# A graph layer with segment maxima: an evenly cut gather list, the bias in another product, and an end in smaller pieces

## The chip, the cores and the metric

The kernel runs on one core of one Trainium2 chip. The metric is the device time of one execution in microseconds (us); lower is better. Its engines are TensorE (PE, with PEld for its weight loads), VectorE (DVE), ScalarE (ACT), GpSimd (POOL) and SyncE (SP, which here only starts DMAs). Each engine works through its own queue in order, and they wait for each other by semaphores.

## The reference

There are 6,250 nodes with 256 features and 100,000 directed edges, sorted by target. For each edge a message is computed, each node takes the maximum of its messages, and the sum with x is normalised:

```python
x_src = x[src]; x_dst = x[dst]
theta_x = (x_dst - x_src) @ theta_w.T + theta_b
phi_x = x_src @ phi_w.T + phi_b
e = relu(theta_x + phi_x)
out = segment_max(e, dst, num_segments=6250)
x = layernorm(x + where(isfinite(out), out, 0.0))
```

The part of a message that depends on the target is the same for all edges of a node. So with b = x @ (phi_w - theta_w)^T and a = x @ theta_w^T, a node's result is relu(a[node] + max over its edges of b[src] + both biases). One row of b for each node suffices, and the work is to take maxima over gathered rows of b.

## The kernel before

**Two parts.** The first 18,688 edges (128 partitions x `T1` = 146 steps) belong to part 1, nodes 0 to 1,129. Each partition walks its own 146 edges: an indirect DMA on GpSimd gathers 128 rows (one step), and VectorE runs a capped maximum over the steps (`run`, L661). The running maxima go to a DRAM table, `maxima_1`, in groups of eight steps (L669); a node's result is read from the place of its last edge. Where a node's edges cross from one partition to the next, `tails_1` and `heads_1` mend the table: `heads_1` gathers the rows at the partitions' first boundaries, takes the maximum with what is carried over (L851) and scatters them back.

Part 2 are the other 5,120 nodes, 40 to a partition. Sources are cut into 17 slots of 375 nodes. For each node and slot one edge at most is chosen (`choice`), and its row comes by a product with a one-hot matrix on TensorE (`slot_part`, L1025): 85 parts of 24 matmuls, with one-hot matrices from ScalarE (L1017, L1018) and VectorE (L1015), and results joined into `acc` by VectorE (L1036). Edges that are left over form a list (`list_pieces`): each partition lists those of its own nodes, at most `LIST` = 288, and walks it as in part 1: 288 gathers (`gather_2`), 288 maxima, 36 writes to `maxima_2`.

**Preparation.** `b_of` transposes x on TensorE, copies it by ScalarE (`x_t`, L710), multiplies it (L720), and VectorE adds the bias and moves the result out of PSUM (L723). It does so for all rows (`b_rows`, in DRAM), and for the first `X_GROUPS` = 4 groups of part 1, whose rows of x are gathered directly since `b_rows` isn't there yet. Meanwhile VectorE fills a table of part 2's edges (`fill_table`), chooses, and forms the list. In the same loops `next_group_1` gathers the other groups of part 1 and starts the first 16 fetch parts.

**The list loop.** For each group of eight steps: eight gathers, the maxima of the group before, and `PACE` = 2.1 fetch parts:

```python
for i in range(LIST // STEPS):
    g, gathers = gather_2(i * STEPS)
    if i:
        run(2, g_before, STEPS, caps_2, (i - 1) * STEPS, maxima_2t, gathers)
    g_before = g
    pace += PACE
    fetch_parts(int(pace))
    pace -= int(pace)
    if i in (3, 5):
        next(heads, None)
```

The loop also finishes part 1's nodes (`rows_of`, `normalise`) in two shares, one node column and eight.

**The end.** Five shares of eight columns of part 2. `rows_of` loads x, gathers a node's row of `maxima_2` (L1127), and for each two columns (a piece) transposes x (L1134), copies it (L1136), multiplies it with theta (L1140), transposes `acc` back (L1149), and VectorE joins all (L1150, L1151, L1154). `normalise` then takes squares (L1165), the root, scales (L1172) and writes the output (L1176), a share behind `rows_of`.

**Order.** The order on each engine is fixed when the program is built, by a planner that places an instruction when its costs say that it can start. The kernel adds order by hand: `in_turn` keeps GpSimd's queue as written, with pauses (`iota` of 160) between gathers; `behind_in_order` places an instruction behind another without a wait. A `run` step of part 2 stands behind the gather of the next group and behind the last `acc` maximum written before it. If the limits of the tables don't hold (`bad`), a general path computes all once more at the end.

## Time and profile before

| what | value |
|---|---|
| median of 3 runs | 854.9 us (851.97 to 855.15) |
| the profiled execution | 852.55 us, its span 850.7 us |
| mean granted TensorE clock | 0.912 |
| PE, PEld busy | 663.9 us (78%), 537.1 us (63%) |
| DVE busy | 673.8 us (79%) |
| ACT busy | 497.8 us (59%) |
| POOL busy | 676.1 us (79%) |
| DMA | 178.69 MB, mean 210 GB/s |

All times are of one profiled execution, counted from the start of its span; the span is shorter than its time because starting and ending lie around it. Busy shares are means over stages that differ, so each stage is read by itself: which engine is full there, and what its successor waits for. Matmuls are pipelined, and a busy PE is not a PE at its peak. A line number names the line of the program that wrote the instruction; L497 is the helper that issues all indirect DMAs.

### The profile page before, as it was taken

What the parts mean: (1) busy time and instruction counts of PE and PEld (TensorE: products, weight loads), DVE (VectorE), ACT (ScalarE), POOL (GpSimd) and SP (SyncE); (2) the same over time, 40 slices, a digit from 0 to 9 for tenths busy, and PEclk for the clock granted to TensorE, in tenths of its full rate; (3) what the DMA queues carried; (4) which work ended last, traced back from release to release, by engine and by line L of the source; (5) the groups of instructions that cost most, each with busy time, mean ns of one, the idle gap of its engine ahead of it and who ended that gap; (6) DMA issues with size and microseconds to landing.
All of it is one profiled execution on the core that took longest, in us unless ns stands there. A gap on an engine that the chain in (4) does not pass through costs nothing. (4 is left out here: it accounts for less than half of the span.)

```text
span 850.7 us, 10236 instructions
## 1 busy us (share of the span) xinstructions
PE 663.9 (78%) x2949; PEld 537.1 (63%) x2949; DVE 673.8 (79%) x1227; ACT 497.8 (59%) x676; POOL 676.1 (79%) x913
## 2 busy tenths in 40 slices
PE   0899983767758285299999999999999999407771
PEld 0688862555536164288888888888888887306660
DVE  4599999977999872389988979888999978517662
ACT  0122224898749246077778868987777775004765
POOL 8796178887888788888888888888888888858820
PEclk9999995998879688599999999999999999758996
DMA  7675347776455663477778857986777667673622
GB/s 231 201 270 200 118 148 249 234 232 189 154 171 174 208 205 111 145 255 251 232 237 268 259 179 241 300 257 208 237 254 246 238 213 265 220 277 94 241 88 102
DMA packets 54353, 178.69 MB, mean 210 GB/s; under 512 B 12416, under 2 KB 13867, under 8 KB 45806
## 3 DMA queue, kind: packets, MB, share of 16 engines
q1 hardware_dynamic: 28306, 105.82, 35.0%
q0 software_dynamic: 23440, 64.42, 26.3%
q10 hardware_dynamic: 2540, 7.69, 2.4%
q8 instruction: 26, 0.43, 0.2%
q14 instruction: 41, 0.34, 0.1%
HBM read 107.88 MB, written 70.80 MB: 210 GB/s over the span
## 5 line engine op out<-in xcount | busy, mean ns | idle before, releaser
L1025 PE MATMUL ps_f<-hot,terms 128*128 128x512 f32 x2040 | 488.6, 400 | 74.5 <-DVE hot L1015 24.6
L1025 PEld LDWEIGHTS ps_f<-hot,terms 128*128 128x128 f32 x2040 | 390.9, 193 | 166.4 <-issue 25.0
L497 POOL DMA_INDIRECT g<-b_rows,list_src x288 | 293.4, 1019 | 50.0 <-issue 46.1
L1017 ACT ACTIVATE hot<-want,minus_row 128x1024 fp32r<-128x1024 f16 x186 | 204.9, 1145 | 133.4 <-PE ps_f L1025 128.5
L661 DVE SCALAR_TENSOR_TENSOR g<-g,caps 128x256 f32<-128x256 f32 x432 | 206.9, 479 | 31.2 <-DMA g<-b_rows,src 14.6
L1036 DVE TENSOR_TENSOR acc<-acc,ps_f 128x1024 f32<-128x1024 f32 x160 | 194.0, 1215 | 38.0 <-PE ps_f L1025 37.4
L497 POOL DMA_INDIRECT g<-b_rows,src x114 | 161.9, 1420 | 59.0 <-issue 29.6
L1018 ACT ACTIVATE hot<-hot 128x1024 fp32r<-128x1024 f32 x186 | 186.1, 1045 | 0.1
L473 POOL IOTA pause<- 128x160 f32 x404 | 125.2, 310 | 4.2
L720 PE MATMUL ps_b<-weights,x_t 128*128 128x256 f32 x324 | 75.8, 386 | 5.1 <-DVE b_sb L723 2.9
L720 PEld LDWEIGHTS ps_b<-weights,x_t 128*128 128x128 f32 x324 | 59.7, 190 | 17.8 <-ACT x_t L710 6.7
L710 ACT COPY x_t<-ps_xt 128x512 f32<-128x512 f32 (+1 forms) x41 | 21.9, 584 | 78.2 <-PE ps_xt L708 78.2
L497 POOL DMA_INDIRECT g<-maxima,place x49 | 48.3, 985 | 15.5 <-issue 15.0
L1140 PE MATMUL ps_e<-weights,x_t 128*128 128x256 f32 x160 | 42.7, 412 | 15.5 <-ACT x_t L1136 15.5
L1015 DVE TENSOR_SCALAR hot<-want,row_id 128x1024 fp32r<-128x1024 f16 x69 | 54.2, 785 | 0.5 <-DMA want<-chosen_rows 0.5
L1136 ACT COPY x_t<-ps_e 128x512 f32<-128x512 f32 x20 | 11.6, 581 | 58.4 <-PE ps_e L1134 58.3
L497 POOL DMA_INDIRECT g<-in_x_dram,src x32 | 38.9, 1215 | 8.7 <-issue 4.7
L1140 PEld LDWEIGHTS ps_e<-weights,x_t 128*128 128x128 f32 x160 | 30.3, 199 | 24.1 <-ACT x_t L1136 20.5
L1150 DVE TENSOR_TENSOR g<-g,ps_e 128x512 f32<-128x512 f32 x20 | 13.7, 686 | 32.1 <-PE ps_e L1149 18.8
L1134 PE MATMUL ps_e<-ident,g 128*128 128x128 f32 x80 | 13.2, 292 | 31.7 <-DVE g L1150 30.5
L1134 PEld LDWEIGHTS ps_e<-ident,g 128*128 128x128 f32 x80 | 10.4, 154 | 32.0 <-DVE g L1150 30.7
L1172 ACT ACTIVATE g<-g,r 128x256 f32<-128x256 f32 x49 | 25.3, 590 | 8.8 <-DVE r L1170 8.8
(210 smaller groups left out, 473.5 us busy)
## 6 DMA issues: line engine op xcount, KB each, us to landing
maxima<-g SPq DMA_DIRECT2D x54, 1024.0 KB
want<-chosen_rows SPq DMA_DIRECT2D x85, 256.0 KB
x_q<-in_x_dram SPq DMA_DIRECT2D x12, 512.0 KB
b_rows<-b_sb ACTq DMA_DIRECT2D x12, 512.0 KB
g<-in_x_dram SPq DMA_DIRECT2D x6, 1024.0 KB
out_dram<-g SPq DMA_DIRECT2D x6, 1024.0 KB
raw<-b_rows SPq DMA_DIRECT2D x16, 336.0 KB
g<-b_rows,list_src POOLq DMA_INDIRECT x288, 4.0
```

The costliest lines, as they stand in the source:

```text
L473: return nc.gpsimd.iota(t, pattern=[[step, t.shape[1]]], base=base, channel_multiplier=per_partition, allow_small_or_imprecise_dtypes=True,)
L497: in_turn(nc.gpsimd.indirect_dma_start(out=out, out_offset=out_offset, in_=in_, in_offset=in_offset))
L661: one = nc.vector.scalar_tensor_tensor(g[:, k, :], last[part], caps[:, t : t + 1], g[:, k, :], op0=ALU.min, op1=ALU.max)
L720: nc.tensor.matmul(ps[:, h, :], x_t[:, h, k, :], weights[:, k, 0, :], start=(k == 0), stop=(k == KC - 1))
L1015: nc.vector.tensor_scalar(hot[:, b, :], want, row_id[:, b : b + 1], None, op0=ALU.is_equal)
L1017: nc.scalar.activation(hot[:, b, :], want, AF.Abs, bias=minus_row[:, b : b + 1], scale=1.0)
L1018: nc.scalar.activation(hot[:, b, :], hot[:, b, :].bitcast(FP), AF.Relu, bias=1.0, scale=-1.0)
L1025: nc.tensor.matmul(ps[:, w : w + 512], terms[:, part, b, h * P : (h + 1) * P], hot[:, b, w : w + 512], start=(i == 0), stop=(i == n - 1),)
L1036: latest_part[0] = nc.vector.tensor_tensor(to, to, ps, op=ALU.max).ins.name
L1134: nc.tensor.transpose(ps[:, 2 * i + c, :], x_f[:, k + i, c * P : (c + 1) * P], ident)
L1140: nc.tensor.matmul(a[:, i, :], x_t[:, 2 * i + c, :], weights[:, c, 1, :], start=(c == 0), stop=(c == KC - 1))
L1172: nc.scalar.activation(x_f[:, k, :], x_f[:, k, :], AF.Identity, bias=mean[:, k : k + 1], scale=inv[:, k : k + 1])
```

## The change

- **Bias.** The sum of both biases is no longer added to b. It is kept in two rows (`bias_terms`, a rounded part and the rest) and added by one more matmul for each node column in `rows_of`, with `pick`, which selects these rows. `b_of` moves its result out of PSUM by a plain ScalarE copy.
- **Six groups of x**, not four, and a ring of six tiles, which the list's gathers share; x in `rows_of` has its own ring of five.
- **Equal chunks.** The partitions' lists are written to DRAM (`list_words`) and cut into 128 chunks of 231 places (`LIST_CHUNK`); a partition walks one chunk and up to 248 places, so that a node that begins in its chunk ends there too. A chunk is pieced together from three owners' lists with three run gathers and two masks. The loop has 31 groups instead of 36; `PACE` is 2.25. A group's maxima lie together in `maxima_2`. The places of nodes (`list_places`) are computed late in the loop.
- **Heads' maximum later.** The gather comes before group 2, the maximum before group 5 and behind the latest GpSimd instruction, the scatter before group 8.
- **The end.** Only part 1's single column is finished in the list loop, its eight others at the end. Pieces of two columns are begun one ahead of the one before; normalisation goes on in steps of two columns between them. The last share of eight is two of four.

The core of the diff (constants, table views, limits and buffers that are only renamed are left out):

```diff
-            nc.vector.tensor_tensor(to, ps[:, :n, :], bias.to_broadcast([P, n, D]), op=ALU.add)
+            nc.scalar.copy(to, ps[:, :n, :])
...
         indirect(heads, maxima_1, in_offset=at_heads)
-        nc.vector.tensor_tensor(heads, heads, carried, op=ALU.max)
         in_turn(iota(pause, 1, 0, 0))
+        yield
+        one = nc.vector.tensor_tensor(heads, heads, carried, op=ALU.max)
+        behind_in_order(one, latest[0], "rows that are there")
         yield
         indirect(maxima_1, heads, out_offset=at_heads)
...
+    def list_chunks():
+        ...
+        nc.tensor.matmul(ps[:, :P], counts, tri, start=True, stop=True)
+        nc.tensor.matmul(ps[:, P : P + 1], tri, n_list, start=True, stop=True)
+        nc.vector.tensor_copy(upper_end, ps[:, :P])
+        nc.vector.tensor_tensor(before, ps[:, P : P + 1], n_list, op=ALU.subtract)
+        ...
+        for i in range(3):
+            nc.vector.tensor_scalar(
+                scratch, upper_end, at_edge, None, op0=ALU.is_le, op1=ALU.add, accum_out=number[:, i : i + 1]
+            )
+            ...
+            nc.vector.scalar_tensor_tensor(up, scratch, FAR, upper_end, op0=ALU.mult, op1=ALU.add)
+            nc.vector.tensor_reduce(ends[:, i + 1 : i + 2], up, AX.X, ALU.min)
+            at_edge = ends[:, i + 1 : i + 2]
...
+        nc.vector.tensor_scalar(done, done, (1 << 20) - 1, None, op0=ALU.bitwise_and)
+        nc.vector.tensor_tensor(done, done, owner.to_broadcast([P, OWN_LIST]), op=ALU.bitwise_or)
+        for first_row, rows in ((0, P), (P, 3)):
+            nc.sync.dma_start(
+                flat(list_words, first_row * OWN_LIST, [[OWN_LIST, rows], [1, OWN_LIST]]), done[:rows, :]
+            )
+        yield
...
+        for i, to in enumerate((list_edges, second, third)):
+            gather_run(to, list_words, run_start[:, i : i + 1])
+        for i, to in enumerate((second, third)):
+            nc.vector.tensor_scalar(mask, edge, ends[:, i + 1 : i + 2], None, op0=ALU.is_ge)
+            nc.vector.copy_predicated(list_edges, mask, to)
...
-        g = ring_2.tile([P, STEPS, D], FP, name="g")
+        g = gathered.tile([P, STEPS, D], FP, name="g")
...
-        x_f = ring_2.tile([P, STEPS, D], FP, name="g")
+        x_f = x_ring.tile([P, STEPS, D], FP, name="x_f")
...
             nc.scalar.copy(x_t[:, : 2 * w], ps[:, : 2 * w])
+            yield
             a = ps_tile().rearrange("p (i d) -> p i d", i=2)
             for i in range(w):
                 for c in range(KC):
                     nc.tensor.matmul(
-                        a[:, i, :], x_t[:, 2 * i + c, :], weights[:, c, 1, :], start=(c == 0), stop=(c == KC - 1)
+                        a[:, i, :], x_t[:, 2 * i + c, :], weights[:, c, 1, :], start=(c == 0), stop=False
                     )
+                nc.tensor.matmul(a[:, i, :], pick, bias_terms, start=False, stop=True)
...
+    class Shares:
+        def step(self):
+            if self.begun is not None:
+                piece, norm = self.begun
+                next(piece)
+                self.begun = None
+                if norm is not None:
+                    self.norms.append(norm)
+                    return
+            for _ in range(2):
+                if self.norms and next(self.norms[0], self) is self:
+                    self.norms.pop(0)
+
+        def add(self, *share):
+            pieces, norm = rows_of(*share, self.ps_tile)
+            for i, piece in enumerate(pieces):
+                next(piece)
+                self.step()
+                self.begun = piece, norm if i == len(pieces) - 1 else None
...
     for i in range(LIST // STEPS):
+        if i in (2, 5, 8):
+            next(heads, None)
         g, gathers = gather_2(i * STEPS)
...
-        if i in (3, 5):
-            next(heads, None)
-        if i > 6 and i % 3 == 0 and (early_shares or waiting):
...
+        if i == LIST // STEPS - 4:
+            list_places()
+            early_share = Shares(misc)
+            early_share.add(*LAST)
+            early_share.finish()
...
+    last_shares = [(2, j, STEPS) for j in range(0, TILES - STEPS, STEPS)]
+    last_shares += [(2, j, STEPS // 2) for j in (TILES - STEPS, TILES - STEPS // 2)]
+    at_end = Shares(lambda: ps_end.tile([P, 2 * D], FP, name="ps_e"))
+    for share in [(1, 0, Q1)] + last_shares:
+        at_end.add(*share)
+    at_end.finish()
```

## The prediction

> **What bounds the kernel now.** First the page's forty slices of 21.3 us; a digit is the busy share in tenths.
>
> ```profile
> PE   0899983767758285299999999999999999407771
> DVE  4599999977999872389988979888999978517662
> POOL 8796178887888788888888888888888888858820
> ```
>
> Four stages: a preparation to about 300 us, where VectorE (DVE) is full; a list stage to 750, where GpSimd (POOL) never rests and TensorE (PE) is full after a hole; a gap; an end where nothing is full. The table of busy time by stretch (columns: span, then PE, PEld, DVE, ACT, POOL, granted clock, DMA share, GB/s) says the same in numbers:
>
> ```profile
> 255.00:300.00 45.00, 24.51 (x96) 18.11 (x94) 40.57 (x69) 27.43 (x28) 36.51 (x26) 0.80 0.56 187
> 300.00:355.00 55.00, 29.30 (x120) 23.47 (x120) 21.00 (x41) 22.15 (x23) 48.25 (x73) 0.75 0.47 142
> 355.00:722.00 367.00, 366.69 (x1614) 302.53 (x1614) 323.05 (x499) 278.20 (x298) 325.67 (x488) 0.99 0.75 244
> 722.00:757.00 35.00, 10.72 (x51) 8.46 (x50) 16.70 (x34) 1.76 (x3) 23.71 (x38) 0.70 0.61 210
> 757.00:834.00 77.00, 51.91 (x272) 42.55 (x272) 47.47 (x156) 42.62 (x117) 50.28 (x80) 0.89 0.47 168
> ```
>
> TensorE is done at 722; GpSimd gathers until 750, and the kernel waits. Who waits for whom names the holes:
>
> ```profile
> DVE heads L851 <- DMA heads<-maxima,head_i: 27.5, 1, 27.5
> PE ps_f L1025 <- DVE hot L1015: 24.6, 1, 24.6
> POOL g L497 <- DVE g L723: 23.4, 1, 23.4
> ```
>
> One VectorE instruction, the heads' maximum, waited from 324 to 351.6 for a gather that GpSimd reached at 348.9; everything behind it on VectorE stood, so TensorE stood 24.6. The third wait, 78 to 101.6, is GpSimd out of rows to gather. The costliest groups (busy us, mean ns) give prices:
>
> ```profile
> L497 POOL DMA_INDIRECT g<-b_rows,list_src x288 | 293.4, 1019 | 50.0 <-issue 46.1 <-DVE g L661 2.4 <-DVE acc L1036 0.8
> L661 DVE SCALAR_TENSOR_TENSOR g<-g,caps 128x256 f32<-128x256 f32 x432 | 206.9, 479 | 31.2 <-DMA g<-b_rows,src 14.6 <-DMA g<-b_rows,list_src 13.2
> L723 DVE TENSOR_TENSOR b_sb<-ps_b,bias 128x512 f32<-128x512 f32 (+1 forms) x25 | 16.6, 668 | 1.4 <-PE ps_b L720 1.4
> L723 DVE TENSOR_TENSOR g<-ps_b,bias 128x512 f32<-128x512 f32 x16 | 10.9, 682 | 1.0 <-PE ps_b L720 1.0
> ```
>
> Last, the chain that ended last (start us, us, what). It hangs on the list's last gather: its maximum, the write to `maxima_2`, then gathers held up beside 1 MB loads of x:
>
> ```profile
> 749.32 2.74 DMA g<-b_rows,list_src
> ...
> 752.15 0.49 DVE g L661
> 752.66 4.73 DMA maxima<-g
> 757.41 0.03 issue
> 757.44 8.27 DMA g<-in_x_dram
> 765.72 0.70 DVE g L1150
> ```
>
> The sum is made on the profiled execution: span 850.7, time 852.55, so 1.85 around it. It lies 2.35 below the median of 854.9.
>
> **Preparation.** Two chains must both be over before the first list gather (300.72 now).
>
> VectorE: 249 us busy of the 266 from 34.5 on. Taking the bias off removes its 41 evictions, which follow one another every 0.60 us (42.85, then 43.45): 24.6. ScalarE takes them: 49 copies at 0.58 (its 128x512 copy, L710) is 28 us on an engine that was busy 14 of 67 us there. If such a copy stands ahead of the next `x_t` copy, TensorE waits up to 1.2 for each of the 25 pairs of the main loop, 29 in all; cover is the 12 us by which the new x gathers outlast `b_rows`. VectorE gains work: `list_chunks` and two predicated copies, some 30 instructions of 0.15 to 0.5, about 6. And it gains a wait. The list goes through DRAM: two writes on SP, which may stand behind `maxima_1` writes (SP was held 10.2 us at 289), three run gathers on GpSimd at 1.4, and a landing (2.6 for the heads' gather). VectorE's predicated copies wait for that, with list words and `acc` maxima behind them; the list gathers wait too. No row shows this round trip. Below: 0, if other VectorE work and gathers fill it; above: 10.2 + 4.2 + 2.6 = 17. I take 9, near the heads' and run rows with a free SP. So 300.7 - 24.6 + 6 + 9 = 291, or 274 if the 17 us of idle goes too.
>
> As a page's figure: the Trainium skill, "DMA: Bandwidth & Descriptors", section "Anatomy of one DMA", speaks against round trips: about 2 us fixed for each transfer, mostly the receipt. Two legs by that are 4 where I have 9, and the time would be 5 shorter.
>
> GpSimd: 32 x gathers end at 78. Two more groups are 16 at 2.25 (20 took 45.1 from 33.2), so to 114, over the old hole. Then 98 gathers, not 114. They went at 1.746 ((300.72 - 101.65)/114): 171, to 285. At the stretch 170 to 213 (mean 1154 ns and 0.30 between) it is 257. TensorE's part of the two groups, eight pairs at 2.33, is 19; it ran to 124 and the first fetch part came at 143, so that is nearly covered.
>
> I take 284 for the first list gather, the slower GpSimd pace, and 262 to 302 as ends.
>
> The row behind the pace: gathers cost 1728 ns in 213 to 255, where VectorE was 100% busy with conversions and shifts, and 1018 in 352 to 725. The Trainium skill, "SBUF — State Buffer", section "Who interferes with whom", gives a mechanism: VectorE's two-port modes lock GpSimd out, and descriptors with it. By it the added masks, predicated copies and cast, some 2 us of VectorE, would block GpSimd for as long, and the time would be 2 longer; by the row all this sits in the 1.746.
>
> **List stage.** GpSimd: 299 indirect DMAs (288, nine for part-1 shares, two for the heads) took 300.7 to 750.6, 1.505 each. Now 248 + 1 + 2: 378, a gain of 72. TensorE decides beside it. ScalarE's one-hots mark the period of a fetch part:
>
> ```profile
> 319.84 2.20 ACT L1017 ACTIVATE hot<-want,minus_row 128x1024 fp32r<-128x1024 f16 x2 [1.35 <-PE ps_f L1025]
> 325.28 2.19 ACT L1017 ACTIVATE hot<-want,minus_row 128x1024 fp32r<-128x1024 f16 x2 [1.35 <-PE ps_f L1025]
> ```
>
> 5.44 a part. From 301.4 to 722.0 TensorE did 70 parts (380.8), the part-1 shares (11.7), stood 24.6 behind the heads, and 3.5 is left. The change puts the heads' maximum behind the gathers of three more groups and moves eight of the nine part-1 columns to the end: 380.8 + 1.6 + 3.5 = 386. A group is 8 x 1.505 = 12.0 on GpSimd and 2.25 x 5.44 = 12.2 on TensorE, so they end together, TensorE last: 284 + 386 = 670, GpSimd about 665. Hidden: 40 maxima less on VectorE (19 us at 479 ns), five 1 MB writes less, and `list_places`, a dozen small instructions at the 28th group; should VectorE lose its slack (88% busy), that is 3 us. A ring of six for the list, not seven that shares of x also used: GpSimd waited only 2.4 for a slot.
>
> **End.** The last eight maxima come behind the last part: 670 + 1.2 + 8 x 0.48 + 4.7 for the write is 680. Meanwhile GpSimd gathers the part-1 share (8 x 1.41 = 11.3, from 665). Part 2 needs two gathers and a landing, 5.4, and x lies loaded in five tiles of its own instead of coming just then: first maximum (L1150's) at 687, 765.7 now. Then twenty pieces. They went at 3.48 (19 steps from 765.72 to 831.83), because TensorE's transposes, the copy and the matmuls of a piece follow in line. Begun a piece ahead, a piece costs TensorE 0.45 + 1.99 + 0.45 and two bias matmuls. No row shows such one; a fetch matmul of 512 columns takes 0.23 and an f32 one of 256 some 0.5, so 0.1 to 0.5; I take 0.12, the nearest in type. That is 3.1; GpSimd has 2.8, ScalarE and VectorE about 2.7. Four engines so close don't mesh fully: 3.3, ends 2.9 and 3.9. 687 + 19 x 3.3 + 2.2 is 752. The tail was 16.7 (833.97 to 850.7); half as many squares and scalings in the last share take off 4, half the output some 1: 12. Span 764, time **766**, against 852.55: preparation -17, list -62, end -8.
>
> **Rivals.**
> - *The preparation gives nothing*: the round trip and the evictions on ScalarE eat the 17 us. For it: VectorE there was 90% busy and waits in order. 783.
> - *The stall comes back*: VectorE's order is fixed beforehand, and a misjudged gather stops it again, at the heads or at the list words. 24.6 more: 791. Against: the maximum now stands 24 gathers (36 us) behind its own.
> - *All at its good end*: 262 at the start, pieces at 2.9: 736.
> - *Slower*: GpSimd becomes slow. With shorter gaps VectorE is fuller beside it, and list gathers go as in 213 to 255: 1.728 + 0.30 = 2.03. 251 of them are 509, 123 more than TensorE's 386: 889. It decides from 1.91 on (386 + 93 over 251). Against: 355 to 722, at 88% VectorE, kept 1.505.
> - *It doesn't do what it says*: the new limits of the list fail, and the general path runs as well. Counted on the reference's inputs, the list has 29,311 edges of at most 29,568, the longest chunk reaches place 243 of 248, the fullest owner 269 of 288. It stays off; if not, its 782 gathers at 1.25 or more (0.95 and 0.30 between, the quickest rows) add 978: 1,744.
>
> **How the numbers follow.** The forecast 0.60, nothing from preparation 0.17, the stall 0.12, the good end 0.05, slow gathers 0.05, the general path 0.01. The start's ends (-22, +18) and the pieces' (-8, +11) with the first two rivals give 738 to 798; beyond lie slow gathers, and the worst sums. Three runs spread over 3.2 us, so about 0.5%, 4 us, is what can be told from no change. Faster: 0.60 + 0.17 + 0.12 + 0.05, less 0.01 for sums that fail together, 0.93; the same 0.01; slower 0.06.
>
> **What would show it.** Right: the first list gather near 284; no wait at the heads above 3 us; TensorE and GpSimd ending within 10 us of each other, near 668; the first part-2 maximum near 687 and pieces 3.3 apart. Wrong: a mean list gather above 1.3 us, VectorE waiting more than 15 us for the list's words, TensorE idle in the list stage, or pieces still 3.5 apart.

## The result, and the profile after

The changed kernel takes 775.58 us (median of 4 runs, 775.42 to 778.11) beside 853.43 for the kernel before: a ratio of 0.9096, 95% interval 0.9064 to 0.9128. The forecast was 766 with a range of 738 to 798. The profiled execution is the slowest of the four: time 778.11, span 776.3, 12.3 beyond the forecast span of 764, of which 2.5 are its distance to the median. The first four runs below (the two of the heads, the first of the evictions, and the tail alone) were made while every kernel, the one before included (883.6 to 925.4), stood at many places with nothing in the trace that released it, so of those four only waits and stretches are read and no total.

The forty slices, of 19.4 us now:

```profile
PE   0989999367777849999999999999999999999980
DVE  5499999999888857698888979889797997867881
POOL 8798887878887855888888888888888888868860
```

The gap in TensorE's row behind the list stage is gone, and so is the hole of the heads. What is left of holes lies in slices 8 to 15, 136 to 291 us. The chain that ended last says the same by engine; in it, TensorE's fetch matmuls (L1053) are 45% of the span:

```profile
PE 47%; POOL 13%; DMA 6%; ACT 5%; DVE 5%; issue 4%; DVEq 0%; POOLq 0%; ACTq 0%
```

Busy time by stretch (span, then PE, PEld, DVE, ACT, POOL with their instructions, granted clock, DMA share, GB/s):

```profile
136.00:164.00 28.00, 8.59 (x29) 5.78 (x30) 26.79 (x75) 10.17 (x32) 22.21 (x20) 0.63 0.74 249
164.00:226.00 62.00, 47.28 (x187) 35.42 (x187) 56.93 (x94) 60.19 (x89) 52.99 (x34) 0.94 0.65 214
226.00:279.00 53.00, 43.09 (x163) 32.91 (x163) 44.73 (x90) 41.01 (x43) 42.77 (x35) 0.85 0.65 199
279.00:300.00 21.00, 11.94 (x42) 9.20 (x41) 11.71 (x34) 8.19 (x9) 5.12 (x9) 0.76 0.57 193
300.00:683.00 383.00, 381.89 (x1686) 314.92 (x1684) 330.23 (x492) 294.39 (x296) 339.68 (x508) 1.00 0.74 238
```

From 300 on TensorE has no hole; before, it has four stretches with holes. The numbers in brackets there count all matmuls, those of the preparation too, and one that crosses a border twice. So the fetch matmuls alone are counted from run to run, by those begun before 300: 85 fetch parts of 24 must be done whatever happens, 2040 in all, and each one begun before 300 shortens what follows by 5.44/24 = 0.227 us. In the changed kernel they are 367. The fetch and the list gathers on GpSimd, over the whole span (ns least, median and most, first and last start us):

```profile
L1053 PE MATMUL ps_f<-hot,terms x367: 387/389/796, 163.6 to 299.9; 128*128 128x512 f32 x184
L1053 PE MATMUL ps_f<-hot,terms x2040: 387/389/796, 163.6 to 682.2; 128*128 128x512 f32 x186
L505 POOL DMA_INDIRECT g<-b_rows,list_src x248: 948/956/1540, 298.7 to 675.0; - x124
```

The waits that answer to the three shown of before:

```profile
POOL g L505 <- DVE list_src L1208: 15.1, 1, 15.1
PE ps_f L1053 <- DVE acc L1064: 15.6, 4, 9.1
PE ps L806 <- DVE hot L804: 10.9, 1, 10.9
DVE heads L873 <- DMA heads<-maxima,head_i: 4.8, 1, 4.8
```

VectorE waits 4.8 us at the heads instead of 27.5. New is GpSimd's wait of 15.1 for the list, with a TensorE wait of 9.1 beside it. VectorE's timeline around it (start us, us, engine, line, what, idle before) shows why:

```profile
281.94 0.48 DVE L669 SCALAR_TENSOR_TENSOR g<-g,caps 128x256 f32<-128x256 f32 x1 [0.99 <-DMA g<-b_rows,src]
288.37 0.44 DVE L1196 COPY_PREDICATED dst_w<-words,dst_w 128x248 int32<-128x248 int32 x1 [5.94 <-DMA dst_w<-list_words,run_start]
...
289.62 2.34 DVE L1064 TENSOR_TENSOR acc<-acc,ps_f 128x1024 f32<-128x1024 f32 x2
...
294.14 0.41 DVE L1207 SCALAR_TENSOR_TENSOR list_src<-wide 128x248 int32<-128x248 int32 x1
...
297.00 1.22 DVE L1064 TENSOR_TENSOR acc<-acc,ps_f 128x1024 f32<-128x1024 f32 x1 [2.24 <-PE ps_f L1053]
298.13 0.28 DVE L1208 TENSOR_SCALAR list_src<-list_src 128x248 int32<-128x248 int32 x1
```

The predicated copy (L1196) waits 5.94 us for the second run gather, which was issued at 280.74 and landed at 288.3. The two `acc` maxima queued behind it came at 289.62, and TensorE, whose last matmul had ended at 281.8, stood until 290.89:

```profile
277.00 4.83 PE L1053 MATMUL ps_f<-hot,terms 128*128 128x512 f32 x20 [2.53 <-DVE acc L1064]
290.89 2.08 PE L1053 MATMUL ps_f<-hot,terms 128*128 128x512 f32 x4 [9.06 <-DVE acc L1064]
```

TensorE in turn was then late with the maximum at 297.00, and this one stood in front of the last instruction of `list_src` (298.13). So each engine waited once for the other, in an order that was fixed beforehand. The way through DRAM, from the write of the list's words (275.45) to the predicated copy, took 12.9 us:

```profile
275.45 0.67 SPq L1184 DMA_DIRECT2D list_words<-work  x2
```

The groups whose prices the forecast used (line, operation and count, busy us, mean ns, idle before):

```profile
L505 POOL DMA_INDIRECT g<-b_rows,list_src x248 | 252.8, 1019 | 55.3 <-issue 38.1 <-DVE list_src L1208 15.1 <-DVE g L669 1.1
L505 POOL DMA_INDIRECT g<-b_rows,src x98 | 136.1, 1388 | 30.0 <-issue 25.9 <-DMA g<-b_rows,src 1.5 <-DVE g L669 0.9
L1251 PE MATMUL ps_e<-bias_terms,pick 128*128 128x256 f32 x48 | 22.5, 468 | 0.0
```

A list gather takes 1019 ns, as before. The bias matmul is the last row. Its 468 ns are not what it costs, since matmuls overlap. That is read from starts, on TensorE's timeline of one piece:

```profile
731.75 1.03 PE L1248 MATMUL ps_e<-weights,x_t 128*128 128x256 f32 x4
732.43 0.47 PE L1251 MATMUL ps_e<-bias_terms,pick 128*128 128x256 f32 x1
732.74 1.02 PE L1248 MATMUL ps_e<-weights,x_t 128*128 128x256 f32 x4
733.41 0.47 PE L1251 MATMUL ps_e<-bias_terms,pick 128*128 128x256 f32 x1
733.72 0.60 PE L1258 MATMUL ps_e<-ident,acc 128*128 128x128 f32 x4
734.15 0.60 PE L1241 MATMUL ps_e<-ident,x_f 128*128 128x128 f32 x4
```

The eight recorded theta matmuls and both bias matmuls take 1.97 us to the next start (731.75 to 733.72). The run without the bias matmuls, below, gives what the eight take alone.

Last the tail, on ScalarE:

```profile
759.13 6.00 ACT L1287 ACTIVATE x_f<-x_f,r 128x256 f32<-128x256 f32 x12 [0.52 <-DVE r L1284]
765.03 0.49 ACT L1277 ACTIVATE squares<-x_f,r 128x256 bf16<-128x256 f32 x1
...
769.04 2.07 ACT L1287 ACTIVATE x_f<-x_f,r 128x256 f32<-128x256 f32 x4 [1.24 <-DVE r L1284]
```

The last sum on VectorE ended at 757.3. The last share's four squares start only at 765.03, behind twelve scalings of the two shares before it.

The first and the last maximum of part 2 at the end (L1259):

```profile
698.67 0.69 DVE L1259 TENSOR_TENSOR g<-g,ps_e 128x512 f32<-128x512 f32 x1 [2.23 <-DMA g<-maxima,place]
...
754.54 0.69 DVE L1259 TENSOR_TENSOR g<-g,ps_e 128x512 f32<-128x512 f32 x1 [0.72 <-PE ps_e L1258]
```

From the end of the list onward, the two kernels divide as follows:

| us | before | forecast | after |
|---|---|---|---|
| the list's last engine done | 750.6 (GpSimd) | 670 (TensorE) | 682.6 (TensorE) |
| from there to the first part-2 maximum | 15.1 | 17 | 16.1 |
| from the first to the last such maximum | 66.1 | 62.7 | 55.9 |
| from there to the end of the span | 18.9 | 14.3 | 21.8 |
| end | 850.7 | 764 | 776.3 |

### The profile page after: what moved, and what is told of

Same layout as the page of the kernel before. It is cut to its first block, busy times and chain, and to the rows that moved or that the text cites. A ratio compares the mean times of both kernels' runs of the same rounds, so it can differ in the third digit from the quotient of the medians.

```text
span 776.3 us, 10452 instructions
## 1 busy us (share of the span) xinstructions
PE 673.0 (87%) x3098; PEld 555.0 (71%) x3098; DVE 644.8 (83%) x1199; ACT 527.7 (68%) x734; POOL 632.5 (81%) x872
## 4 chain that ended last, share of the span: by engine, by line
PE 47%; POOL 13%; DMA 6%; ACT 5%; DVE 5%; issue 4%; DVEq 0%; POOLq 0%; ACTq 0%
PE ps_f L1053 45%; POOL g L505 12%; DMA g<-b_rows,src 3%; ACT x_f L1287 2%; ACT squares L1277 2%; POOL pause L481 1%; DMA dst_w<-list_words,run_start 1%; DVE g L669 1%; DMA maxima<-g 1%; DVE acc L1064 1%; DMA g<-b_rows,list_src 1%; PE ps_e L1248 1%; DMA g<-maxima,place 1%; DVE x_f L1263 1%; PE ps L806 0%
## 5 line engine op out<-in xcount | busy, mean ns | idle before, releaser
L1053 PE MATMUL ps_f<-hot,terms 128*128 128x512 f32 x2040 | 482.1, 397 | 39.5 <-DVE acc L1064 15.6
L1053 PEld LDWEIGHTS ps_f<-hot,terms 128*128 128x128 f32 x2040 | 388.3, 192 | 129.4 <-ACT hot L1046 24.4
L505 POOL DMA_INDIRECT g<-b_rows,list_src x248 | 252.8, 1019 | 55.3 <-issue 38.1
L669 DVE SCALAR_TENSOR_TENSOR g<-g,caps 128x256 f32<-128x256 f32 x392 | 188.1, 480 | 16.8 <-DMA g<-b_rows,src 13.0
L505 POOL DMA_INDIRECT g<-b_rows,src x98 | 136.1, 1388 | 30.0 <-issue 25.9
L740 PE MATMUL ps_b<-weights,x_t 128*128 128x256 f32 x388 | 89.0, 383 | 3.5 <-ACT x_t L730 2.6
L740 PEld LDWEIGHTS ps_b<-weights,x_t 128*128 128x128 f32 x388 | 72.0, 190 | 16.0 <-ACT x_t L730 7.0
L505 POOL DMA_INDIRECT g<-in_x_dram,src x48 | 61.2, 1276 | 11.3 <-issue 7.1
L743 ACT COPY b_sb<-ps_b 128x512 f32<-128x512 f32 (+1 forms) x25 | 14.4, 578 | 31.6 <-PE ps_b L740 24.1
L743 ACT COPY g<-ps_b 128x512 f32<-128x512 f32 x24 | 14.1, 586 | 29.8 <-PE ps_b L740 28.2
L1287 ACT ACTIVATE x_f<-x_f,r 128x256 f32<-128x256 f32 x49 | 25.3, 589 | 8.6 <-DVE r L1284 8.6
L1277 ACT ACTIVATE squares<-x_f,r 128x256 bf16<-128x256 f32 x49 | 24.3, 499 | 0.7 <-DVE r L1274 0.7
```

Of the source, the lines that this page charges most:

```text
L505: in_turn(nc.gpsimd.indirect_dma_start(out=out, out_offset=out_offset, in_=in_, in_offset=in_offset))
L669: one = nc.vector.scalar_tensor_tensor(g[:, k, :], last[part], caps[:, t : t + 1], g[:, k, :], op0=ALU.min, op1=ALU.max)
L740: nc.tensor.matmul(ps[:, h, :], x_t[:, h, k, :], weights[:, k, 0, :], start=(k == 0), stop=(k == KC - 1))
L1053: nc.tensor.matmul(ps[:, w : w + 512], terms[:, part, b, h * P : (h + 1) * P], hot[:, b, w : w + 512], start=(i == 0), stop=(i == n - 1),)
L1277: nc.scalar.activation(squares, x_f[:, k, :], AF.Square, bias=mean[:, k : k + 1], scale=1.0, accum_out=var[:, k : k + 1])
L1287: nc.scalar.activation(x_f[:, k, :], x_f[:, k, :], AF.Identity, bias=mean[:, k : k + 1], scale=inv[:, k : k + 1])
```

## The experiments

The theory at this point: TensorE bounds the list stage. Its end is late by the two things that kept it from fetching before 300, the pairs of the two added groups of x and the hole at the list's words, and the last stretch is ScalarE's backlog. From the list's way through DRAM on, and for the evictions' second run, the runs come from two later sessions, in which the kernel before took 853.11 and 851.22 us; the changed kernel was not repeated there, so a difference from its 775.58 holds some 2 us that may be the session's. By their ratio to the kernel before, the intervals of the hole alone (0.9000 to 0.9069) and of the run without the way through DRAM (0.8978 to 0.9065) just touch the changed kernel's, and those of four groups of x (0.8972 to 0.9054) and of the parts together lie clear below it.

**The heads' maximum, both ways.** Alone, on the kernel before:

```diff
-        nc.vector.tensor_tensor(heads, heads, carried, op=ALU.max)
         in_turn(iota(pause, 1, 0, 0))
+        yield
+        one = nc.vector.tensor_tensor(heads, heads, carried, op=ALU.max)
+        behind_in_order(one, latest[0], "rows that are there")
...
-        if i in (3, 5):
+        if i in (2, 5, 8):
```

> The kernel before, with one part of the change alone: the heads' maximum is put behind the gathers of three more groups of the list. Theory (GpSimd set the end of the list there: 299 gathers at 1.505 us, TensorE finished 28 us ahead of it at 722): the 24.6 us stall of TensorE goes, TensorE is done near 697 instead of 722, the last list gather stays near 750 and the time stays within 3 us of 853.4. Rival (the stall was on the path): 853.4 - 24.6 = about 829.

Its total (892.16 beside 916.05) can't be used. Inside the list stage the wait is 4.3 us instead of 27.5, and TensorE's last fetch matmul starts at 714.6 instead of 721.7; the list gathers run as they did, from 302.7 to 751.5, or 448.8 (before: 448.6):

```profile
DVE heads L853 <- DMA heads<-maxima,head_i: 4.3, 1, 4.3
```

The list gathers of this run by their tile (ns least, median and most, first and last start):

```profile
L497 POOL DMA_INDIRECT g<-b_rows,list_src x288: 948/956/1568, 302.7 to 751.5; - x144
```

So, as the theory has it, TensorE's gain stays in front of a GpSimd that ends 37 us after it. By this trace, this part of the change alone has nothing to shorten. The theory's 697 for TensorE was missed: of the 24.6 us only 7.1 arrived. TensorE waited another 8.1 us for one-hots of VectorE, and ScalarE stood 25.2 us with nothing in the trace that released it; how much of this belongs to the session is open.

The reverse, the old order (maximum right behind its gather, i in 3 and 5) in the changed kernel:

> The changed kernel with that part undone: the heads' maximum stands directly behind its own gather again and is issued two groups sooner in VectorE's order. Theory (in the changed kernel TensorE sets the end of the list stage, 352 of 353 us busy, and GpSimd ends 6.6 us ahead): VectorE waits 20 to 28 us for the heads' gather, TensorE stands nearly as long, and the time is 775.6 + 20 = about 796 (790 to 803). Rival (GpSimd still bounds): within 6 us of 775.6.

The wait is 18.5 us, by the waits of this run:

```profile
DVE heads L871 <- DMA heads<-maxima,head_i: 18.5, 1, 18.5
```

TensorE stands for 15.15 of them, by its timeline:

```profile
343.37 2.07 PE L1051 MATMUL ps_f<-hot,terms 128*128 128x512 f32 x4 [15.15 <-DVE acc L1062]
```

Its last fetch matmul then starts 22.3 us after the start of the last list gather (703.7 against 681.4). In the changed kernel it is 7.2 (682.2 against 675.0), and the 15.1 between them are the hole. So, by the traces, the heads' part is worth about 15 us once the list is cut, and nothing before. The total of this run (845.67) is not usable either, and the theory's 796 stays untested.

**The evictions back on VectorE.**

```diff
-            nc.scalar.copy(to, ps[:, :n, :])
+            nc.vector.tensor_copy(to, ps[:, :n, :])
```

> The changed kernel with the evictions of x theta^T (and of the x groups) copied from PSUM by VectorE instead of ScalarE, 49 copies of about 0.60 us; the bias stays out of them. Theory (VectorE sets when the list's words are ready in the preparation): the first list gather comes 20 to 29 us later than 298.7, and the time is near 798 (790 to 805). Rival (by 279 GpSimd's 98 gathers bind, and the words were ready 2 us ahead of them, so VectorE has little to lose or gain): 775 to 783.

In this run (882.19) the engines stood, with nothing in the trace that released them, just between 140 and 230, the stage in question; it says nothing. It was run again:

> The run evict_dve once more, since in the first the engines stood for their instructions at many places. The changed kernel with the 49 evictions of x theta^T copied by VectorE instead of ScalarE. Theory (VectorE's order sets when fetch parts begin and when the list's words are ready): TensorE's first fetch part and the first list gather come 15 to 29 us later, and the time is 788 to 803. Rival (VectorE stands idle 24 of 186 us between 113 and 299, enough to take most of it): 775 to 783.

787.54 us (785.41 to 789.40), 12.0 more than the changed kernel and half a microsecond under the range of the theory. The list's words come later on VectorE: GpSimd waits for them ahead of the run gathers, where the changed kernel has no such wait, and the first list gather is at 313.9 instead of 298.7, as the theory had it:

```profile
POOL dst_w L505 <- DVE place_f L815: 20.6, 1, 20.6
```

The stretch before it:

```profile
279.00:300.00 21.00, 16.49 (x59) 12.51 (x58) 20.54 (x34) 15.38 (x16) 1.29 (x2) 0.84 0.46 171
```

The list gathers by their tile:

```profile
L505 POOL DMA_INDIRECT g<-b_rows,list_src x248: 948/956/1537, 313.9 to 688.7; - x124
```

In the stretch GpSimd is nearly idle (1.29 us) and VectorE full (20.54). GpSimd starts its last list gather at 688.7, TensorE its last fetch matmul at 691.7: 15 us on the start of the list cost 9.5 at its end. The theory's other half missed: the first fetch part was to come 15 to 29 us later too, and it came at 154.1, 9.5 earlier than in the changed kernel. So TensorE had begun more fetch matmuls before 300 (383) and still ended later: here the list, which began 15 us later, kept GpSimd busy until 688.7. The 24.6 us of evictions taken off VectorE were worth 12.

**The list's way through DRAM.** Left out, so that each partition walks the first 248 entries of its own owner's list and other edges are gathered:

```diff
-        for i, to in enumerate((list_edges, second, third)):
-            gather_run(to, list_words, run_start[:, i : i + 1])
-        for i, to in enumerate((second, third)):
-            nc.vector.tensor_scalar(mask, edge, ends[:, i + 1 : i + 2], None, op0=ALU.is_ge)
-            nc.vector.copy_predicated(list_edges, mask, to)
+        nc.vector.tensor_scalar(list_edges, done[:, :LIST], (1 << 27) - 1, None, op0=ALU.bitwise_and)
```

> The changed kernel without the list's way back from DRAM: the three run gathers and the two predicated copies are left out, and each partition walks the first 248 entries of its own owner's list instead of its equal chunk (so other edges are gathered; the two writes to list_words stay). Theory (behind the run gathers GpSimd stood 15.1 us and the gathers themselves took 4.2; VectorE's wait for their landing also stopped the acc maxima and with them TensorE for 9.1): the first list gather comes 12 to 19 us sooner after the last gather of b_rows, TensorE does not stand 9.1 us behind acc, and the time is 775.6 - 9 to 15 = 761 to 767. Rival (the list words were late anyway, VectorE's order decides): within 4 us of 775.6.

770.37 us (767.26 to 771.76), 5.2 less: between theory and rival. The first list gather is at 287.4, 11.3 earlier, and TensorE begins 405 fetch matmuls before 300 instead of 367; it starts its last one at 673.9 instead of 682.2. GpSimd still stood 8.9 us after its last gather of `b_rows`, for VectorE's instructions on the list. In the changed kernel it is 19.7 us from that gather's end to the first list gather. So 8.9 of these are VectorE's own work and order, and the other 10.8 went with the run gathers and the copies that wait for them, a little less than the 12 to 19 of the theory.

**Two repairs together.** The first predicated copy behind the `acc` maxima, two fetch parts later in exchange, and the last shares' squares on VectorE. The second edit was also run alone, among the first four runs, where its few microseconds can't be seen (847.23):

```diff
-PACE = 2.25
+PACE = 2.3
...
-            nc.vector.copy_predicated(list_edges, mask, to)
+            one = nc.vector.copy_predicated(list_edges, mask, to)
+            if i == 0:
+                behind_in_order(one, latest_part[0], "VectorE's order")
...
+            if n == STEPS // 2:
+                nc.vector.scalar_tensor_tensor(
+                    squares, x_f[:, k, :], mean[:, k : k + 1], x_f[:, k, :],
+                    op0=ALU.add, op1=ALU.mult, accum_out=var[:, k : k + 1],
+                )
+                continue
...
+            if n == STEPS // 2 and j0 == TILES - n and k < 2:
+                nc.vector.tensor_scalar(
...
-        if i % 2:
+        if i % 2 and i < 10:
             next_group_1(1)
```

> The changed kernel with the last two shares of four columns normalised by VectorE in part: their squares as one multiply-add with a sum on VectorE, two of the very last four scalings on VectorE, and four tiles instead of two for the means and variances. Theory (the 19 us behind the last sum are ScalarE's backlog: 12 squares, 12 scalings, then the last 4 and 4 in line, and the last mean stood for a tile that those scalings held): ScalarE loses 8 squares of 0.49 and 2 scalings of 0.5, and the last squares no longer wait for 12 scalings, so the span ends 5 to 9 us sooner, 767 to 771. Rival (GpSimd's gathers or TensorE's pieces set the end and the tail only follows): within 2 us of 775.6.

> The changed kernel with two repairs that leave its work as it is. First, VectorE's order around the list: the first predicated copy is put behind the acc maxima of the fetch part that stood 9.1 us in front of TensorE, and two fetch parts are begun behind the list instead of in front (the pace is 2.3 instead of 2.25 for that). Second, the edit of the run 'tail'. Theory (two holes are the whole miss: the list begins 5 us sooner and TensorE loses 9.1 us less, and the tail is 5 to 9 us shorter): 775.6 - 6 - 7 = about 762 (757 to 767). Rival (the gather's landing sets the list's begin, whatever stands ahead of it, and GpSimd then sets the end): 767 to 771.

776.19 us (773.89 to 777.74) against 775.58: nothing came of either, and the theory missed as it was put. The list does begin at 293.7, 5 us sooner, but TensorE starts its last fetch matmul at 681.5, as in the changed kernel: with two parts put off it had begun 368 fetch matmuls before 300, the changed kernel 367. The tail's edit ran into the order again:

```profile
755.84 0.49 DVE L1280 SCALAR_TENSOR_TENSOR squares<-x_f,r 128x256 bf16<-128x256 f32 x1 [1.44 <-ACT squares L1285]
...
761.57 6.00 ACT L1300 ACTIVATE x_f<-x_f,r 128x256 f32<-128x256 f32 x12 [0.82 <-DVE r L1292]
```

VectorE's squares share their buffers with ScalarE's. The first waited for one, stood ahead of the last piece and held it up (4.07 us behind the piece before it, not 2.94), and the twelve scalings still stood together.

**The hole alone.** The same predicated copy behind the same maxima, with no part put off:

```diff
+            if i == 8:
+                part_before = latest_part[0]
...
+            one = nc.vector.copy_predicated(list_edges, mask, to)
+            if i == 0:
+                behind_in_order(one, part_before, "VectorE's order")
```

> The changed kernel with one edit: on VectorE the first predicated copy of the list stands behind the acc maxima of the fetch part that was ready before it (they stood 9.1 us behind the copy's wait for the run gathers). No fetch part is begun later, unlike in order_tail. Theory (the list stage is set by the holes in TensorE's fetch parts, wherever they lie, not by when the list begins): the 9.1 us hole goes, TensorE ends the fetch 7 to 9 us sooner, GpSimd's list is then level with it, and the time is 767 to 770. Rival (as in order_tail the hole only moves: TensorE stands for hots or for later acc maxima instead): 774 to 778.

770.57 us (768.78 to 772.61), 5.0 less and half a microsecond above the theory's range. Beside the two repairs it is the cleanest pair: the list begins at 293.7 there and at 293.0 here, yet TensorE's last fetch matmul starts at 681.5 there and 8.0 sooner here, at 673.5. The stretch of the hole now holds 74 matmuls instead of 42:

```profile
279.00:300.00 21.00, 16.88 (x74) 12.87 (x73) 17.60 (x55) 14.84 (x16) 9.26 (x14) 1.00 0.65 212
```

Of the fetch matmuls, 399 are begun before 300:

```profile
L1053 PE MATMUL ps_f<-hot,terms x399: 387/389/797, 163.2 to 299.9; 128*128 128x512 f32 x200
```

That is 32 more than 367, or 7.3 us by 0.227; 8.7 arrived. As long as GpSimd ends ahead of TensorE, when the list begins hardly matters; what TensorE has fetched by then does.

**Four groups of x.**

```diff
-X_GROUPS = 6
+X_GROUPS = 4
```

> The changed kernel with four groups of x instead of six (all else as it is). Theory (the two more groups fill the time in which GpSimd waits for b_rows): GpSimd stands again 15 to 23 us for b_rows near 78 to 101, then needs 114 gathers at 1.69 = 193, so the first list gather comes 10 to 18 us later, and the time is 786 to 793. Rival (VectorE sets when the list's words are ready, so GpSimd's gathers end early enough either way and TensorE saves 19 us of pairs): within 5 us of 775.6.

769.27 us (767.34 to 774.47), 6.3 less: against the theory, and just beyond the rival. GpSimd does wait again:

```profile
POOL g L505 <- DMA b_rows<-b_sb: 19.3, 1, 19.3
```

But the list begins at 299.3 all the same, and TensorE, with four pairs less for each group left out, begins its fetch parts at 143.8 instead of 163.6:

```profile
136.00:164.00 28.00, 21.22 (x79) 15.83 (x80) 26.85 (x72) 26.25 (x40) 22.05 (x23) 0.79 0.95 320
```

That is 79 matmuls where the changed kernel has 29 in the same stretch; of the fetch matmuls, 408 are begun before 300. These are 41 more, or 9.3 us, of which 6.1 arrived: GpSimd's last list gather starts at 676.5 and TensorE's last fetch matmul at 676.1, level now. The two groups fill 19 us of an engine that was not the bound and cost the one that is.

**Fewer fetch parts.** The last 7 of 85 parts left out:

```diff
+    del parts[-7:]
```

> The changed kernel without its last 7 fetch parts of 85 (their rows are left out of the maxima). Theory (in the list stage TensorE and GpSimd are nearly level, GpSimd ending 6.6 us ahead): 38 us of TensorE's time go but the time falls only by 6 to 9, to 767 to 770, with GpSimd then setting the list's end. Rival (TensorE alone bounds, and GpSimd's gathers are faster when VectorE and TensorE leave it alone): 775.6 - 20 to 38 = 738 to 756.

786.77 us (784.24 to 788.20), 11 more for 8% less fetch work; neither side had that. List gathers keep their pace (295.2 to 670.4), which speaks against the rival. TensorE ended its parts at 639.6, and VectorE, in its fixed order, then stood 31.57 us for the part-1 rows, which GpSimd gathers only behind its whole list (from 671.8), with the list's maxima queued behind:

```profile
676.24 0.69 DVE L1260 TENSOR_TENSOR g<-g,ps_e 128x512 f32<-128x512 f32 x1 [31.57 <-DMA g<-maxima,place]
700.80 0.95 POOL L505 DMA_INDIRECT g<-maxima,place  x1 [17.70 <-DMA maxima<-g]
```

The write of `maxima_2` came late, and the first part-2 gather started at 700.8 instead of 694.2. It is the heads' stall in another place. How far the time would fall in an order fit for fewer parts stays open.

**Without the bias matmuls of the end**, so without the bias:

```diff
-                        a[:, i, :], x_t[:, 2 * i + c, :], weights[:, c, 1, :], start=(c == 0), stop=False
+                        a[:, i, :], x_t[:, 2 * i + c, :], weights[:, c, 1, :], start=(c == 0), stop=(c == KC - 1)
...
-                nc.tensor.matmul(a[:, i, :], pick, bias_terms, start=False, stop=True)
```

> The changed kernel without the two matmuls with pick in each piece of the end, so without the bias. Theory (a piece of 2.94 us is TensorE's 2.9, but GpSimd's gathers stand right behind it at 8 x 1.41 for four pieces, 2.82): pieces at 2.8 and the time 772 to 774. Rival (TensorE alone sets the pieces): 20 x 0.6 = 12 less, 763 to 766.

773.69 us (770.58 to 777.21), in the theory's range; but 1.9 less than 775.58 is no more than the sessions differ by, so the total shows only that the rival's 12 are not there. The rival's price was too high as well. TensorE's timeline has the eight theta matmuls alone:

```profile
727.52 1.89 PE L1248 MATMUL ps_e<-weights,x_t 128*128 128x256 f32 x8
729.25 0.60 PE L1257 MATMUL ps_e<-ident,acc 128*128 128x128 f32 x4
```

They take 1.73 to the next start, where eight and two bias matmuls took 1.97: a bias matmul adds 0.12 us, not the 0.30 that the rival counts, and forty are 4.7 us. Of these, first to last part-2 maximum got 1.1 (54.8 instead of 55.9). Without them a piece is 2.6 for TensorE, and GpSimd's two gathers at 1.41 are 2.8. Up to the end this kernel is the changed one, and yet its list began 1.8 us sooner (296.9) and its last fetch matmul 2.3 (679.9); in the run with fewer parts, the same up to there, the list began at 295.2. That is how far profiles of the same work lie apart here.

**The parts that paid, together.** Five groups of x, the edit of "hole", and a tail in which VectorE works only behind its last sum and in a buffer of its own:

```diff
-X_GROUPS = 6
+X_GROUPS = 5
...
+            if last_4:
+                squares = work.tile([P, D], BF, name="squares_4", bufs=1)
+                behind_the_sums(nc.vector.scalar_tensor_tensor(
...
+            if last_8 and (k < 2 or not last_4):
+                behind_the_sums(nc.vector.tensor_scalar(
```

> The changed kernel with three edits that leave its work as it is: five groups of x (with six, the last x gathers end at 112 and TensorE begins its fetch parts at 164; with four, GpSimd waited 19 us for b_rows until 97.6 and TensorE began at 144); the edit of 'hole'; and in the last eight columns VectorE scales the first four and squares the last four, behind the last sum, so that ScalarE's twelve scalings become eight. Theory (TensorE's start and holes set the list's end, ScalarE's queue the tail): fetch parts begin near 153, and 775.6 - 6 - 5 - 5 = about 760 (755 to 765). Rival (GpSimd's 378 us of list gathers bind as soon as TensorE gains, and the tail's wait moves to the square root behind the eight scalings): 767 to 771.

767.41 us (762.32 to 769.21), ratio to the kernel before 0.8990 (0.8951 to 0.9028): below the changed kernel's 0.9096, with no overlap of the intervals. The median is the rival's, and two of its reasons are seen. TensorE's fetch began at 153.9 and had begun 440 matmuls before 300, 73 more than 367 or 16.6 us, of which 10.8 arrived; from 300 to 683 it was busy 376.86 of 383. GpSimd's last list gather starts at 671.6 and TensorE's last fetch matmul at 671.4: level. ScalarE's timeline at the end:

```profile
750.63 4.04 ACT L1310 ACTIVATE x_f<-x_f,r 128x256 f32<-128x256 f32 x8 [1.86 <-DVE r L1302]
754.57 0.19 ACT L413 ACTIVATE r<-r 128x4 f32<-128x4 f32 x1
```

The last square root (L413) does stand behind the eight scalings. Still, from the last maximum (744.69) to the end (762.7) it is 18.0 instead of 21.8.

Side by side, the runs bear the theory out as far as GpSimd leaves room for it (last two columns: last start):

| run | fetch matmuls begun before 300 | first list gather | list gather on GpSimd | fetch matmul on TensorE |
|---|---|---|---|---|
| changed | 367 | 298.7 | 675.0 | 682.2 |
| two repairs | 368 | 293.7 | 671.3 | 681.5 |
| without the bias | 375 | 296.9 | 673.1 | 679.9 |
| the hole | 399 | 293.0 | 671.3 | 673.5 |
| no way through DRAM | 405 | 287.4 | 663.8 | 673.9 |
| four groups of x | 408 | 299.3 | 676.5 | 676.1 |
| parts together | 440 | 294.9 | 671.6 | 671.4 |
| evictions on VectorE | 383 | 313.9 | 688.7 | 691.7 |

In the first five rows TensorE's end follows the fetch count, to about 1 us, whatever the first list gather. In the last three it does not. When their list begins, 408, 418 and 442 fetch matmuls are begun, 351 to 376 in the first five: the fetch is so far ahead that the list is the later one, and TensorE waits for one-hots of VectorE, which runs the list's maxima too (5.0, 4.7 and 8.3 us in the list stage, 0.9 in the changed kernel). No run puts the old, longer list back into the changed kernel; that its cut is the largest gain is read from the two traces.

## Why the prediction was right, and where its steps failed

The direction and the mechanism held: the list on GpSimd went from 449.9 to 377.7 us (1.505 for each of 251 indirect DMAs, as taken), TensorE became the bound by a small margin (GpSimd done at 676.4, TensorE at 682.6; 665 and 670 were forecast), and the heads' wait went to 4.8, a little over the 3 allowed. The list stage on TensorE took 384 from the first list gather, where 386 was taken. The x gathers ended at 112.4 (114), the gathers of `b_rows` went at 1.69 (1.746). None of the four signs of being wrong was seen.

The miss of 12.3 in the span is three terms: 11.7 late at the first part-2 maximum (698.7 against 687), 6.8 less for the pieces, 7.5 more for the tail. That the pieces made up for over half of the late start is luck, since the two have nothing to do with each other.

*The start.* "I take 284 for the first list gather": 298.7. The 9 us for the round trip were in the sum of VectorE's chain, but GpSimd's chain, 285, was taken to end the stage, as if the trip could lie beside it. Only its first leg did: the words were written at 275.45, beside the last gathers of `b_rows`, but the run gathers are queued behind these, so that they, their landing and VectorE's work on the list came behind GpSimd's 279.0: 19.7 to the first list gather. The trip itself took 12.9 for the 9. As a place to start the sum from, the first list gather was only half the matter. Between the run without the hole and the two repairs, the list begins within 0.7 us and the fetch ends 8.0 apart; with the evictions on VectorE it begins 15.2 later and the fetch ends 9.5 later. TensorE's fetch work is the other half, and there a second step failed: "TensorE's part of the two groups ... is nearly covered". It is not: the first fetch part moved from 143.5 to 163.6, and taking the two groups out gave 6.3 back. With the evictions on VectorE and all six groups it came at 154.1, so the two groups' pairs are not all of these 20 us; what the rest is stays open. The hole behind the predicated copy is the other loss, 5.0.

*The preparation's gain.* 17 us were forecast for it, most of them from the evictions. At the first list gather 2.0 arrived. The evictions did pay, 12.0 by the run that puts them back, and the trip with its order and the two groups of x took that away again. The rival "the preparation gives nothing" describes the start; the time came out below its 783 because the list stage began 2.0 sooner and ran a little shorter and the pieces were nearly at their best end (2.94 for 2.9), which the longer tail took back only in part.

*The stall.* The rival "the stall comes back ... at the list words" is what happened, on a smaller scale: 15.1 for GpSimd and 9.1 for TensorE, where it priced 24.6.

*The end.* Pieces were put at 3.3 because "four engines so close don't mesh fully". They took 2.94 each. Begun a piece ahead, they do mesh: a piece is 2.84 us for TensorE from start to start (731.75 to 734.59), and its matmuls stand in line. The sum for a piece, 3.1, was too long in the theta matmuls: 1.99 is the length of a row that ends with the recorded length of its last matmul, while from start to start the eight take 1.73. The 0.12 for a bias matmul was right. The tail was "12", by counting half the squares and scalings of the last share; it was 19.0 from the last sum, because ScalarE came to it just at the end of twelve squares (757.6) and with twelve scalings of the two shares before still to do (759.13 to 765.1). That the normalisation piled up because the pieces are closer together is likely, but no run shows it.

*Slips in the sums.* 284 and 378 are 662 for GpSimd, not 665; 680 and 5.4 are 685.4, not 687; and the good end's 736 lies outside the range that begins at 738. None of them decides.

*The pages.* By the Trainium skill, "DMA: Bandwidth & Descriptors", "Anatomy of one DMA", two legs would be 4 us, an estimate (the section is on DMAs that GpSimd issues; the first leg here goes by SP). Here the second run gather alone took 7.5 us from issue to landing, and the heads' gather 2.7 in the kernel before (348.9 to 351.6) and 6.9 in the changed one. By the Trainium skill, "SBUF — State Buffer", "Who interferes with whom", VectorE's added work would hold GpSimd up; the section names copies, casts and `tensor_scalar`, so it covers the masks and the cast of the prediction's 2 us and does not name predicated copies. The gathers of `b_rows` kept 1.69 us each over their stage, also in the run with the evictions on VectorE (97 from 115.4 to 279.0), so the 2 us don't show in the sum. Within a stretch, slow gathers do go with a full VectorE: between 226 and 279 that run had VectorE busy 52.9 us and 27 gathers of 1.75 us each, the changed kernel 44.7 us and 34 of 1.25. That the one causes the other is not shown.

## What to carry to other kernels

When a change moves the bound from one engine to another, start the sum anew from the work of the new bound: what it must do, when it can begin, and every hole ahead of the stage, since each is paid at the end as long as the old bound leaves room. An instruction that waits on a round trip belongs behind whatever the busiest engine is waiting for, and an order that is fixed beforehand must be read again after each change in the amount of work, less work included. What a matmul costs is read from start to start, with it and without it, and not from its recorded length. A tail that is counted from the last share alone leaves out the backlog of the engine that does it.

## What was not expected of the hardware

A matmul with `pick` (its operands fp32r, 256 columns) among f32 matmuls is recorded with 468 ns, starts 0.03 us after the f32 matmul before it and 0.30 before the next, and adds 0.12 us to the sequence; a recorded f32 matmul of 256 columns adds 0.216. Of three run gathers of 248 words for each partition, issued 1.4 us apart, the second needed 7.5 us to land.
